# A decoder layer with attention and experts: first loads on two queues, where VectorE's large pieces lie in a step, and the order of the last output products

## Chip, cores and metric

The kernel runs on one core of a Trainium2 chip. The metric is the device time of one execution in microseconds; before the change the median of three runs is 1617.37 us (1615.99 to 1620.86). Traces come from one profiled execution of 1619.34 us, whose span from first to last instruction is 1617.6 us.

## What is computed

The input is x of shape (4, 512, 512): four batches of 512 rows, all in f32. The layer has three parts, each on a layer norm of the running sum:

```python
x = x + attention(layernorm(x), wq, wk, wv, wo)   # 32 query heads, 8 key heads of 64, rope, causal
x = x + quantized_product(layernorm(x), ctx)      # rows and ctx rounded to fp8 in blocks of 128
x = x + moe(layernorm(x), Wg, W1, W3, W2, sw1, sw3, sw2)

# moe, with T = 2048 rows, 8 experts, 256 places each, H = 704
eidx = argmax(softmax(xt @ Wg));  pos = place of the row in its expert's list
out  = gate * expert(eidx)(xt) if pos < 256 else 0
out += (silu(xt @ sw1) * (xt @ sw3)) @ sw2        # shared expert, for all rows
```

## The kernel before

**Engines.** TensorE (PE) does products and transposes, VectorE (DVE) and ScalarE (ACT) empty its banks, GpSimd (POOL) does rotation sums, divisions by softmax sums and additions to the running sum. Transfers are issued from ScalarE's queue (`bulk`, L102) and SP's queue. PSUM has 4 banks for scores and their transposes (`sp`), 1 for values' products (`av`), 3 for everything else (`mm`).

**The start** (L147 to L214, L1017 to L1043). Four row blocks of the first batch are loaded on ScalarE's queue, the rope tables on SP's, then weights of keys, queries and values. 40 dummy transposes (`spin`) run meanwhile. Then: statistics of the rows (`job_hs`), the rope tables' transposes into `rt`, 12 more dummies, then `job_h` (rows transposed), one key product, three query products and the first values' product.

**The step loop** (L1118 to L1133). Attention runs in 80 steps, 20 for each of the 4 batches; five steps treat four pairs of heads. Step `d` stands for two half steps `n = 2d` and `n + 1`. In a step the program writes down:

1. `scores` of the *next* step: the products of queries and keys into `sp` banks; VectorE takes each row's extreme and masks (`pm`, `mn`, L948), ScalarE takes exponentials (L958);
2. `weighted`: values' products of pairs that are ready (`av`, copied by ScalarE);
3. first half of the filler, `work.upto(n, ...)`;
4. `turned`: transposes of this step's probabilities (`pt`, L975), copied to `pT` by ScalarE (L986) and VectorE (L992);
5. second half of the filler, `work.upto(n + 1, ...)`.

Each engine takes its instructions in this written order.

**The filler.** All other work of the loop is cut into jobs: Python generators that write instructions and yield. Their keys: `q`, `k`, `v` (projections), `r` (reciprocals of softmax sums), `m` (their use on three quarters of a group), `o` (output product of a group of 8 heads), `c`, `cs` (rounding of ctx), `hs`, `h` (rows of the next batch), `s`, `t` (norm and quantized product), `w` (norm, router, scatter). The class `Fill` chooses: by due step, by what must be over (with a lag in halves of a step, `HALF` = 7250 ns), then by rank `want`. A yield of a positive number is time of TensorE in ns by the author's count; a negative one asks for a pause in halves; `"dve"` or `"quiet"` with a size asks for that much VectorE time in one piece, `"quiet"` also for GpSimd to be idle. `upto(n, pace, room, busy)` fills a half until TensorE's share `pace` is spent; pieces for VectorE are taken while `room` lasts (3.2 us in the first half, 4.4 in the second, L1127 and L1133). Jobs named in `CHAIN` (L720) are looked at first.

A group's output product `job_o` first writes the fourth quarter's division (`over_sums(b, a, 3)`), then pauses, then 16 products. It needs `wo`, whose tile has one buffer (L133), loaded once the group before is over.

**The tail.** After the loop, jobs left over are written between units of the shared expert (`units`, L1244 to L1267; `between` gives VectorE 2.5 us of room). When no job is left, three more units follow, then the experts, then what units remain, between groups of four rows that are gathered, combined and stored (L1353 to L1371). How many units remain depends on when the jobs end.

Of the kernel before, what the change touches and what calls it, by code (L numbers as in the profile page):

```python
# [8 lines left out]
F32 = mybir.dt.float32  # L9
# [14 lines left out]
def decoder_layer(  # L24
# [107 lines left out]
    def load_o(b, a):  # L132
        w = am2.tile([P, 4, D], F32, tag="wo", name=f"wo_{b}_{a}")  # L133
        bulk(
            out=w, in_=wo[a * 512 : (a + 1) * 512, :].rearrange("(r p) n -> p r n", p=P)
        )
        wts["o", a] = w
# [3 lines left out]
    def load_h(b):  # L141
        for j in range(TB):
            i = b * TB + j
            rows[b, j] = pj.tile([P, D], F32, tag="h", bufs=4, name=f"h_{b}_{j}")
            bulk(out=rows[b, j], in_=xf[i * P : (i + 1) * P, :])

    load_h(0)  # L147

    ident = const.tile([P, P], F32, name="ident")
# [12 lines left out]

    spin(40, "a")

# [15 lines left out]
    nc.sync.dma_start(out=rp, in_=rope.rearrange("(i p) c d -> p i c d", p=P))  # L180
    wts["v0"] = tile_v(0)
    load_k(0, 0)
    load_q(0, 0)
    load_v(0)

# [171 lines left out]
    def job_r(b, a):  # L357

        rr = am2.tile([P, 32], F32, tag="rr", bufs=2, name=f"rr_{b}_{a}")
        nc.vector.reciprocal(rr, rss[b, a])  # L360
        yield -0.6
        pt = bank("mm", f"prr_{b}_{a}")
        nc.tensor.transpose(pt[0:32, 0:P], rr, ident)
        rrT = am2.tile([32, P], F32, tag="rrT", bufs=2, name=f"rrT_{b}_{a}")
        nc.scalar.copy(rrT, pt[0:32, 0:P])
        yield 110
        n = b * NG + a
        bulk(out=rrd[n], in_=rrT)
        yield -0.6
        while n and over.get(("rrb", *divmod(n - 1, NG)), 1e18) + 0.7 * HALF > work.at:  # L370
            yield -0.2
        rrb = am2.tile([P, 4, T], F32, tag="rrb", name=f"rrb_{b}_{a}")
        rrbs[b, a] = rrb
        rows = rrd[n].rearrange("(r g i) q -> g r (i q)", r=4, g=2)
        for g in range(2):
            bulk(out=rrb[g * HD : (g + 1) * HD, :, :], in_=rows[g].partition_broadcast(HD))
# [5 lines left out]
    def job_m(b, a):  # L382
# [3 lines left out]
        yield 0  # L386

    def job_o(b, a):

        aT = aTs[b, a]  # L390
        over_sums(b, a, 3)
        over["rrb", b, a] = work.at
        yield -0.6
# [74 lines left out]
    def pace(b):  # L468

        return 1 if b < B - 1 else 0.5  # L470
# [33 lines left out]
    def job_c(b):  # L504
# [27 lines left out]
        for nt in range(TB + 1):  # L532
            if nt < TB:
                yield "quiet", 0.6, 2.4
                load_c(nt + 2)
                qs.append(quantize_round(vs[nt], f"c{b}_{nt}"))
                if nt < TB - 1:
                    scaled(nt + 1)
            else:
                yield -0.8  # L540
            if nt:
                turn(nt - 1)
                yield 220
# [11 lines left out]
    def job_t(b, j):  # L555
# [6 lines left out]
        block_max(am, h)  # L562
        yield "quiet", 0, 1.4
        inv, sx = block_scales(am, ACT_EPS, KC, f"x{b}_{j}", "x")
        cT, sw = cTs[b]

# [6 lines left out]
        )  # L573
        yield -0.5 * pace(b)
        v = quantize_scale(h, inv, f"x{b}_{j}")
        yield "quiet", 1 * pace(b), 2.4
        q = quantize_round(v, f"x{b}_{j}")
        yield -1 * pace(b)
        hT = bp.tile([P, KC, P], BF16, tag="h2T", bufs=2, name=f"h2T_{b}_{j}")
# [26 lines left out]
    def job_w(b):  # L606
# [14 lines left out]
        over["acc", b] = work.at  # L621
        yield -0.8 * pace(b)
        def small(tag, n=E, dt=F32):
# [95 lines left out]

    CHAIN = ("h", "hs", "cs", "c", "s", "t", "w")  # L720

# [16 lines left out]
    for b in range(B):  # L738
        z = b * SPB
        before = [(("acc", b - 2), 0.7)] if b > 1 else []  # L740
        add(z + 2, 0, ("x", b), load(load_x, b), *before)
        if b:
            add(z - 18, 0, ("wv", b), load(load_v, b), (("q", b - 1, 11), 0.5))
            add(z - 24, 0, ("hx", b), load(load_h, b), *([(("zero",), 0.7)] if b == 1 else []))
            add(z - 22, 0, ("hs", b), job_hs(b), (("hx", b), 1))
            add(z - 16, 1760, ("h", b), job_h(b), (("hs", b), 1), (("q", b - 1, 4 * NG - 1), 0))
        for j in range(TB):
# [5 lines left out]
        for a in range(NG):  # L753
# [17 lines left out]
            for r, due in enumerate((-9.5, -8.5, -7, -5)):  # L771
# [7 lines left out]
            n = b * NG + a  # L779
            before = [(("o", *divmod(n - 1, NG)), 0.7)] if n else []  # L780
            add(za + 5, 0, ("wo", b, a), load(load_o, b, a), *before)
            add(za + 7, 110, ("r", b, a), job_r(b, a))
            add(za + 8, 0, ("m", b, a), job_m(b, a), (("r", b, a), 1.5), want=za + 3)
            add(
                za + 10, 4 * MM4, ("o", b, a), job_o(b, a),
                (("wo", b, a), 1.5), (("x", b), 1), (("m", b, a), 0),
                want=za + (21, 21 if b < B - 1 else 18.5, 17, 16.5)[a],
            )
# [16 lines left out]
    class Fill:  # L805
# [4 lines left out]
        def first(self, n, room=0.0, chain=False):  # L810
            for i, job in enumerate(jobs):
                if job.key[0] in CHAIN:
                    if not room and self.at < self.cool:
                        continue
                elif chain:
                    continue
# [30 lines left out]

        def upto(self, n, pace, room=0.0, busy=0):

            self.cool = max(self.cool, self.at + busy)  # L850
            while True:

                spent, job = self.spent, self.first(n, room) if room > 0 else None
                if job:
# [3 lines left out]
                    if self.spent == spent:  # L858
                        continue
                elif self.spent >= pace:  # L860
                    return
                if self.spent < pace:

                    job = self.first(n, chain=True)
                    while job:
                        job = self.step(job, n)
                    if self.now is None:
# [152 lines left out]
    for c in range(2):  # L1020
        for half in range(2):
# [3 lines left out]
                rp[:, :, c, lo : lo + HH].unsqueeze(2).to_broadcast([P, TB, 2, HH]),  # L1025
            )
    rt = pj.tile([P, 2, T], F32, name="rt")
    for c in range(2):
# [7 lines left out]
        nc.scalar.copy(rt[:, c, :], pt)  # L1036
    spin(12, "b")
    for gen in (
        job_h(0), job_k(0, 0), job_q(0, 0), job_q(0, 1), job_q(0, 2), job_v(0, 0)
    ):  # L1040
        for _ in gen:
            pass
# [6 lines left out]

    even[B - 1] -= 4 * MM4 / SPB  # L1050

# [66 lines left out]
    for d in range(len(todo)):  # L1118
# [133 lines left out]
    def between():  # L1252
        work.at += 1720
        work.upto(n, 1e18, 2.5)

# [177 lines left out]
```

## Time and profile before

| what | value |
|---|---|
| median of three runs | 1617.37 us (1615.99 to 1620.86) |
| profiled execution, its span | 1619.34 us, 1617.6 us |
| granted TensorE clock over the span | 0.988 |
| step loop, first to last transposes of probabilities | 43.4 to 1100.7 us |
| experts | about 1323 to 1566 us |
| HBM traffic | 102 GB/s over the span |

The page's rows read: instruction group by line, engine, operation and tiles, count, busy us and mean ns; then the engine's idle time just before them and what ended it. Such rows for the operations that the change moves:

```profile
L443 DVE TENSOR_TENSOR qv_x<-qv_x,qm_x 128x512 f32<-128x512 f32 x16 | 16.8, 1048 | 0.6
L445 DVE TENSOR_TENSOR qq_x<-qv_x,qm_x 128x512 bf16<-128x512 f32 x16 | 15.3, 959 | 0.5
L568 DVE TENSOR_TENSOR sxw<-sf_c,sf_x 128x16 f32<-128x16 f32 x16 | 11.7, 728 | 0.6
L593 DVE TENSOR_TENSOR y<-py,sxw 128x512 f32<-128x512 f32 x64 | 42.9, 688 | 51.8 <-PE py L591 28.3 <-POOL acc L268 17.0 <-PE av L1006 3.7
```

A step is best read from a timeline of TensorE between two groups of `pt` transposes: sixteen records of about 0.11 us each.

### The profile page before, as it was taken

What the parts mean: (1) busy time and instruction counts of PE and PEld (TensorE: products, weight loads), DVE (VectorE), ACT (ScalarE), POOL (GpSimd) and SP (SyncE); (2) the same over time, 40 slices, a digit from 0 to 9 for tenths busy, and PEclk for the clock granted to TensorE, in tenths of its full rate; (3) what the DMA queues carried; (4) which work ended last, traced back from release to release, by engine and by line L of the source; (5) the groups of instructions that cost most, each with busy time, mean ns of one, the idle gap of its engine ahead of it and who ended that gap; (6) DMA issues with size and microseconds to landing.
All of it is one profiled execution on the core that took longest, in us unless ns stands there. A gap on an engine that the chain in (4) does not pass through costs nothing. (4 is left out here: it accounts for less than half of the span.)

```text
span 1617.6 us, 19823 instructions
## 1 busy us (share of the span) xinstructions
PE 1568.9 (97%) x6659; PEld 858.7 (53%) x6664; DVE 838.9 (52%) x2399; ACT 518.1 (32%) x1541; POOL 336.3 (21%) x293
## 2 busy tenths in 40 slices
PE   8999999999999998999999999989999999999998
PEld 5555554554545554454455554555444547767753
DVE  4466644478767456877745595765445211111113
ACT  2445443444444434333434444351100101101100
POOL 2031220214432030324303132322033000000012
PEclk9999999999999999999999999989999999999999
DMA  4373341353523253332515251246050253546427
GB/s 138 122 233 102 94 128 27 105 157 86 143 87 98 59 143 115 89 99 67 148 49 159 87 131 53 58 148 200 20 206 32 73 190 130 182 155 237 140 77 262
DMA packets 118918, 195.32 MB, mean 121 GB/s; under 512 B 17184, under 2 KB 36640, under 8 KB 118304
## 3 DMA queue, kind: packets, MB, share of 16 engines
q10 hardware_dynamic: 65760, 101.46, 21.7%
q1 hardware_dynamic: 50496, 84.20, 16.7%
q0 software_dynamic: 2560, 8.39, 1.6%
q8 instruction: 53, 0.87, 0.2%
q14 instruction: 49, 0.40, 0.1%
HBM read 136.07 MB, written 28.57 MB: 102 GB/s over the span
## 5 line engine op out<-in xcount | busy, mean ns | idle before, releaser
L958 ACT ACTIVATE pm<-pm,mn 128x256 f32<-128x256 f32 (+3 forms) x512 | 281.9, 553 | 362.4 <-DVE mn L948 322.8
L948 DVE CUSTOM_DVE_ANT_0 pm<-sc,mask 128x256 f32<-128x256 f32 (+3 forms) x512 | 217.1, 486 | 103.0 <-PE sc L925 102.7
L397 PE MATMUL py<-wo,aT 128*128 128x512 f32 x512 | 243.9, 610 | 3.2 <-POOL aT L268 1.7
L303 PE MATMUL psq<-hT,wq 128*128 128x512 f32 x512 | 236.6, 598 | 2.2 <-DVE y L593 1.7
L925 PE MATMUL sc<-kT,t1q 64*128 64x384 f32 (+3 forms) x1024 | 173.8, 455 | 12.8 <-DVE pT L992 5.5
L268 POOL TENSOR_TENSOR t1q<-t1q,tsq 128x512 f32<-128x512 f32 x64 | 83.5, 1305 | 437.5 <-DMA tsq<-t2q 243.6
L992 DVE COPY pT<-pt 128x128 f32<-128x128 f32 (+3 forms) x256 | 114.1, 485 | 108.8 <-PE pt L975 100.6
L975 PEld LDWEIGHTS pt<-ident,pm 128*128 128x128 f32 x1280 | 147.0, 143 | 39.3 <-issue 30.8
L975 PE MATMUL pt<-ident,pm 128*128 128x128 f32 x1280 | 156.4, 276 | 2.2 <-DVE pT L992 0.9
L986 ACT COPY pT<-pt 128x128 f32<-128x128 f32 (+3 forms) x256 | 98.6, 431 | 186.5 <-PE pt L975 160.2
L1006 PE MATMUL av<-pT,v 128*64 128x512 f32 (+3 forms) x1024 | 156.6, 448 | 0.0
L1167 PE MATMUL p_s<-h3x,slot_s 128*128 128x512 f32 x352 | 156.2, 595 | 0.0
L1167 PE MATMUL p_e<-xT,slot_e 128*128 128x256 f32 x704 | 155.1, 380 | 0.0
L303 PEld LDWEIGHTS psq<-hT,wq 128*128 128x128 f32 x512 | 91.7, 190 | 100.8 <-issue 95.8
L1167 PEld LDWEIGHTS p_e<-xT,slot_e 128*128 128x128 f32 x704 | 132.6, 190 | 23.2 <-issue 5.8
L397 PEld LDWEIGHTS py<-wo,aT 128*128 128x128 f32 x512 | 92.5, 192 | 96.0 <-issue 84.7
L925 PEld LDWEIGHTS sc<-kT,t1q 64*128 64x128 f32 x1024 | 87.5, 188 | 98.0 <-issue 64.7
L1006 PEld LDWEIGHTS av<-pT,v 128*64 128x64 f32 x1024 | 69.5, 139 | 110.5 <-issue 97.7
L268 POOL TENSOR_TENSOR acc<-acc,y 128x512 f32<-128x512 f32 x64 | 81.5, 1279 | 180.0 <-DVE y L593 179.0
L1167 PEld LDWEIGHTS p_s<-h3x,slot_s 128*128 128x128 f32 x352 | 65.5, 190 | 75.7 <-issue 73.7
L958 ACT ACTIVATION_READ_ACCUMULATOR pm<-pm,mn 128x1 f32 x512 | 96.9, 189 | 0.0
L268 POOL TENSOR_TENSOR aT<-aT,rrb 128x512 f32<-128x512 f32 x64 | 82.7, 1318 | 26.0 <-DMA rrb<-rrd 26.0
(174 smaller groups left out, 1362.7 us busy)
## 6 DMA issues: line engine op xcount, KB each, us to landing
slot_e<-in_L_ffn_W_dram SPq DMA_DIRECT2D x14, 1280.0 KB
wq<-in_L_attn_wq_dram ACTq DMA_DIRECT2D x16, 1024.0 KB
tsq<-t2q SPq DMA_DIRECT2D x256, 64.0 KB
wo<-in_L_attn_wo_dram ACTq DMA_DIRECT2D x16, 1024.0 KB
rrb<-rrd ACTq DMA_DIRECT2D x32, 512.0 KB
slot_e<-in_L_ffn_W_dram SPq DMA_DIRECT2D x7, 1408.0 KB
kT<-t1k ACTq DMA_DIRECT2D x64, 128.0 KB
xt<-x SPq DMA_DIRECT2D x28, 256.0 KB
```

Source lines behind the costliest of these rows:

```text
L268: nc.gpsimd.tensor_tensor(*args)
L303: nc.tensor.matmul(ps, w[:, k, c0 : c0 + P], hTs[b][:, k, :], start=(k == 0), stop=(k == KC - 1),)
L397: nc.tensor.matmul(py, aT[:, r, j * P : (j + 1) * P], wts["o", a][:, r, :], start=(r == 0), stop=(r == 3),)
L925: nc.tensor.matmul(scs[g][:, o : o + nk], qTs[b, p][g * HD : (g + 1) * HD, it * P : nk], kTs[b, p // 2][g * HD : (g + 1) * HD, 0:nk], star ...
L948: nc.vector.tensor_tensor_reduce(out=pm[:, o : o + nk], in0=scs[g][:, o : o + nk], in1=mask[:, T - nk : T], scale=-(HD**-0.5), scalar=3.0e ...
L958: nc.scalar.activation(pm[:, o : o + nk], pm[:, o : o + nk], AF.Exp, bias=mn, scale=-1.0, accum_out=rss[b, a][:, col : col + 1],)
L975: nc.tensor.transpose(pt[:, j * P : (j + 1) * P], pms[g][:, j * P : (j + 1) * P], ident)
L986: nc.scalar.copy(pT[:, 0 : it + 1, it * P : nk], pt[:, o : o + nk].rearrange("p (j t) -> p j t", t=P),)
L992: nc.vector.tensor_copy(pT[:, it + 1, 0:nk], pt[:, o : o + nk])
L1006: nc.tensor.matmul(av[g * HD : (g + 1) * HD, j * P : T], vs[b][:, j, v0 : v0 + HD], rhs, start=(j == 0), stop=(j == TB - 1),)
L1167: nc.tensor.matmul(pp[:, 0:cols], w13[:, k, o : o + P], xT[:, k, 0:cols], start=(k == 0), stop=(k == KC - 1),)
```

## The change

At the start, row blocks 1 and 3 of the first batch are loaded on SP's queue, ahead of the rope tables; the weights of values and keys are asked for right after the rows. The 12 later dummies join the first 40. The first batch's row transposes and first values' product are written before the rope tables' transposes.

In the loop, `upto` gets a limit `most` for one piece of VectorE: 1.35 us in the first half of a step, 9.0 in the second. Chain jobs are now looked at in each round, also when TensorE's share is spent, and with them jobs outside the chain that have no TensorE work left; `r`, `m` and the new `n` are chain jobs. `n` holds the fourth quarter's division, taken out of `job_o`. Sizes and pauses of several pieces are changed; the scale products `sxw` of a row block are written after its rounding.

For the last batch, the third group's output weights get a buffer of the values' tile, the order of its groups' output products is given by other ranks, and the share of filler per step is lowered by 7 products of 3.44 us rather than 4. In the tail VectorE's room is 2.8.

```diff
     def load_o(b, a):
-        w = am2.tile([P, 4, D], F32, tag="wo", name=f"wo_{b}_{a}")
+        if b == B - 1 and a == NG - 2:
+            w = am1.tile([P, 4, D], F32, tag="v", bufs=2, name=f"wo_{b}_{a}")
+        else:
+            w = am2.tile([P, 4, D], F32, tag="wo", name=f"wo_{b}_{a}")
...
-            bulk(out=rows[b, j], in_=xf[i * P : (i + 1) * P, :])
+            issue = nc.sync.dma_start if not b and j % 2 else bulk
+            issue(out=rows[b, j], in_=xf[i * P : (i + 1) * P, :])
     load_h(0)
+    wts["v0"] = tile_v(0)
+    load_v(0)
+    load_k(0, 0)
...
-    spin(40, "a")
+    spin(52, "a")
...
-    wts["v0"] = tile_v(0)
-    load_k(0, 0)
     load_q(0, 0)
-    load_v(0)
...
     def job_r(b, a):
+        late = 1 if b * NG + a < B * NG - 2 else 0.6
+        yield "dve", 0, 0.4
         nc.vector.reciprocal(rr, rss[b, a])
-        yield -0.6
+        yield -0.9 * late
...
-    def job_o(b, a):
-        aT = aTs[b, a]
+    def job_n(b, a):
         over_sums(b, a, 3)
         over["rrb", b, a] = work.at
-        yield -0.6
+        yield 0
+    def job_o(b, a):
+        aT = aTs[b, a]
...
-        yield "quiet", 0, 1.4
+        yield "quiet", 0, 1.0
         inv, sx = block_scales(am, ACT_EPS, KC, f"x{b}_{j}", "x")
+        yield -0.5 * pace(b)
+        v = quantize_scale(h, inv, f"x{b}_{j}")
+        yield "quiet", 1 * pace(b), 2.7
+        q = quantize_round(v, f"x{b}_{j}")
         cT, sw = cTs[b]
...
-        yield -0.5 * pace(b)
-        v = quantize_scale(h, inv, f"x{b}_{j}")
-        yield "quiet", 1 * pace(b), 2.4
-        q = quantize_round(v, f"x{b}_{j}")
-        yield -1 * pace(b)
+        yield -1.2 * pace(b)
...
-    CHAIN = ("h", "hs", "cs", "c", "s", "t", "w")
+    CHAIN = ("h", "hs", "cs", "c", "s", "t", "w", "r", "m", "n")
...
             before = [(("o", *divmod(n - 1, NG)), 0.7)] if n else []
+            if b == B - 1 and a > 1:
+                before = [(("o", b, 1), 0.7)] if a == 3 else []
...
-                (("wo", b, a), 1.5), (("x", b), 1), (("m", b, a), 0),
-                want=za + (21, 21 if b < B - 1 else 18.5, 17, 16.5)[a],
+                (("wo", b, a), 1.5), (("x", b), 1), (("n", b, a), 0.6),
+                want=za + ((21, 21, 17, 16.5) if b < B - 1 else (22, 19.5, 18, 16.5))[a],
...
-                elif chain:
+                elif chain and job.left > 0:
                     continue
...
-        def upto(self, n, pace, room=0.0, busy=0):
+        def upto(self, n, pace, room=0.0, busy=0, most=9.0):
...
-                spent, job = self.spent, self.first(n, room) if room > 0 else None
+                spent, job = self.spent, self.first(n, min(room, most)) if room > 0 else None
...
-                elif self.spent >= pace:
+                job = self.first(n, chain=True)
+                if job is None and self.spent >= pace:
                     return
+                while job:
+                    job = self.step(job, n)
...
-    spin(12, "b")
-    for gen in (
-        job_h(0), job_k(0, 0), job_q(0, 0), job_q(0, 1), job_q(0, 2), job_v(0, 0)
-    ):
+    for gen in (job_k(0, 0), job_q(0, 0), job_q(0, 1), job_q(0, 2)):
...
-    even[B - 1] -= 4 * MM4 / SPB
+    even[B - 1] -= 7 * MM4 / SPB
...
-        work.upto(n, goal, 3.2, 1900)
+        work.upto(n, goal, 3.2, 1900, 1.35)
...
-        work.upto(n, 1e18, 2.5)
+        work.upto(n, 1e18, 2.8)
```

Left out are pauses in `job_c` (0.8 to 1.3) and `job_w` (0.8 to 1.2), a later load of the running sum, and earlier ranks for `r` and `m`; and that `job_h(0)` and `job_v(0, 0)` now run ahead of the tables' transposes.

More of the change, by code (lines that the diff above doesn't have):

```diff
@@ L368, in job_r @@
         bulk(out=rrd[n], in_=rrT)
-        yield -0.6
+        yield -0.6 * late
         while n and over.get(("rrb", *divmod(n - 1, NG)), 1e18) + 0.7 * HALF > work.at:
@@ L386, in job_m @@
         yield 0
+    def job_n(b, a):
+        over_sums(b, a, 3)
+        over["rrb", b, a] = work.at
+        yield 0
     def job_o(b, a):
         aT = aTs[b, a]
-        over_sums(b, a, 3)
-        over["rrb", b, a] = work.at
-        yield -0.6
         for j in range(TB):
@@ L539, in job_c @@
             else:
-                yield -0.8
+                yield -1.3
             if nt:
@@ L621, in job_w @@
         over["acc", b] = work.at
-        yield -0.8 * pace(b)
+        yield -1.2 * pace(b)
         def small(tag, n=E, dt=F32):
@@ L740, in decoder_layer @@
         before = [(("acc", b - 2), 0.7)] if b > 1 else []
-        add(z + 2, 0, ("x", b), load(load_x, b), *before)
+        add(z + 5, 0, ("x", b), load(load_x, b), *before)
         if b:
@@ L745, in decoder_layer @@
             add(z - 22, 0, ("hs", b), job_hs(b), (("hx", b), 1))
-            add(z - 16, 1760, ("h", b), job_h(b), (("hs", b), 1), (("q", b - 1, 4 * NG - 1), 0))
+            add(z - 16, 1760, ("h", b), job_h(b), (("hs", b), 1.5), (("q", b - 1, 4 * NG - 1), 0))
         for j in range(TB):
@@ L780, in decoder_layer @@
             before = [(("o", *divmod(n - 1, NG)), 0.7)] if n else []
+            if b == B - 1 and a > 1:
+                before = [(("o", b, 1), 0.7)] if a == 3 else []
             add(za + 5, 0, ("wo", b, a), load(load_o, b, a), *before)
-            add(za + 7, 110, ("r", b, a), job_r(b, a))
-            add(za + 8, 0, ("m", b, a), job_m(b, a), (("r", b, a), 1.5), want=za + 3)
+            add(za + 7, 110, ("r", b, a), job_r(b, a), want=za - 20)
+            add(za + 8, 0, ("m", b, a), job_m(b, a), (("r", b, a), 1.5 if n < B * NG - 2 else 1), want=za - 20)
+            add(za + 10, 0, ("n", b, a), job_n(b, a), (("m", b, a), 0), want=za - 20)
             add(
                 za + 10, 4 * MM4, ("o", b, a), job_o(b, a),
-                (("wo", b, a), 1.5), (("x", b), 1), (("m", b, a), 0),
-                want=za + (21, 21 if b < B - 1 else 18.5, 17, 16.5)[a],
+                (("wo", b, a), 1.5), (("x", b), 1), (("n", b, a), 0.6),
+                want=za + ((21, 21, 17, 16.5) if b < B - 1 else (22, 19.5, 18, 16.5))[a],
             )
@@ L859, in upto @@
                         continue
-                elif self.spent >= pace:
+                job = self.first(n, chain=True)
+                if job is None and self.spent >= pace:
                     return
+                while job:
+                    job = self.step(job, n)
                 if self.spent < pace:
-                    job = self.first(n, chain=True)
-                    while job:
-                        job = self.step(job, n)
                     if self.now is None:
@@ L1026, in decoder_layer @@
             )
+    for gen in (job_h(0), job_v(0, 0)):
+        for _ in gen:
+            pass
     rt = pj.tile([P, 2, T], F32, name="rt")
```

## Prediction

> **What bounds the kernel now.** I read the page's busy shares first, then windows of TensorE, then its timeline at the worst windows. The share says that TensorE is the bound, and also how little there is to win: 1617.6 - 1568.9 = 48.7 us idle.
>
> ```profile
> PE 1568.9 (97%) x6659; PEld 858.7 (53%) x6664; DVE 838.9 (52%) x2399; ACT 518.1 (32%) x1541; POOL 336.3 (21%) x293
> ```
>
> Idle is not the whole loss: after gaps the granted clock halves for a while. To count both I took a rule from the trace. I cut the step loop (80 steps, numbered from 0) at the first transpose of each step's probabilities (`pt`, L975) and counted, from the order of TensorE's instructions, the filler between two cuts: a product 128x512 in f32 costs 0.86 us (two records of 429 ns), in bf16 0.22, a row block's four transposes 0.44 or 0.22. An undisturbed step lasts filler + 6.16 us (scores 2.1, values' product 2.3, transposes 1.75), or 3.86 in each fifth step, which has no values' product. The next view gives busy us by engine, then the clock: rows 1 and 4 are undisturbed steps (11 fillers, 9.46 + 6.16 = 15.62), the others the worst.
>
> ```profile
> core 0: us, PE busy (x) PEld busy (x) DVE busy (x) ACT busy (x) POOL busy (x), PEclk, DMA share, GB/s
> 241.25:256.87 15.62, 15.62 (x68) 7.94 (x67) 6.15 (x19) 5.85 (x18) 0.00 (x0) 1.00 0.23 50
> 629.33:647.27 17.94, 12.76 (x57) 6.58 (x57) 10.27 (x41) 8.26 (x28) 2.31 (x2) 0.81 0.27 87
> 658.01:678.65 20.64, 17.89 (x75) 8.56 (x74) 18.31 (x39) 7.42 (x25) 11.27 (x9) 0.92 0.25 56
> 1018.59:1034.21 15.62, 15.62 (x67) 7.77 (x66) 12.70 (x30) 5.29 (x16) 5.92 (x5) 1.00 0.23 52
> 1050.11:1059.14 9.03, 6.71 (x50) 4.48 (x48) 8.88 (x16) 1.53 (x4) 5.33 (x4) 1.00 0.09 32
> 1059.14:1067.55 8.41, 7.07 (x32) 4.98 (x33) 5.66 (x26) 7.90 (x29) 0.00 (x0) 0.80 0.61 202
> 1067.55:1081.42 13.87, 12.72 (x45) 6.63 (x47) 5.01 (x20) 6.82 (x23) 0.00 (x0) 0.63 0.63 182
> 1081.42:1088.97 7.55, 7.04 (x48) 4.44 (x47) 5.33 (x17) 4.86 (x15) 2.55 (x2) 1.00 0.40 123
> ```
>
> Row 4 is busy on VectorE (12.70 of 15.62) and loses nothing; the last rows are not and lose most. So what matters is whether TensorE has filler while it waits, and what stands ahead of the evacuations that it waits for. In the window at 629.33 (step 44, one 0.11 us filler) TensorE's timeline shows:
>
> ```profile
> 629.33 1.91 PE L975 MATMUL pt<-ident,pm 128*128 128x128 f32 x16
> 633.91 1.63 PE L925 MATMUL sc<-kT,t1q 64*128 64x256 f32 x10 [2.68 <-DVE pT L992]
> 638.05 2.07 PE L925 MATMUL sc<-kT,t1q 64*128 64x128 f32 x6 [2.50 <-DVE mn L948]
> ```
>
> VectorE did the 13 small operations of a root before the copies `pT`, then a row's scales before the next maxima `mn`.
>
> Losses by the rule (duration - filler - constant, router products counted too), 66.8 us: steps 74 to 77 38.9 - 23.5 = **15.3** (almost no filler left); 44: 17.94 - 9.60 = **8.3**; 46, 49, 51: **12.9**; 35, 36, 55, 56: **9.5** (transposes wait behind exponentials on ScalarE); 65, 70, 71: **4.4**; twelve small ones in 1 to 33, 52, 53: **16.4**. Outside: at the start TensorE waits for the first rows; at the end DMA and VectorE outlast it:
>
> ```profile
> 12.04 2.09 PE L252 MATMUL ptr_h<-ident,h 128*128 128x128 f32 x16 [2.32 <-DVE h L246]
> 14.87 3.70 PE L303 MATMUL psk<-hT,wk 128*128 128x512 f32 x8 [0.74 <-ACT hT L294]
> ...
> 1609.61 2.17 DVE L1344 SCALAR_TENSOR_TENSOR xt<-og,gk,xt 128x512 f32<-128x512 f32 x3 [2.06 <-DMA xt<-x]
> 1612.18 0.75 DVE L1344 SCALAR_TENSOR_TENSOR xt<-og,gk,xt 128x512 f32<-128x512 f32 x1 [0.40 <-DMA xt<-x]
> 1612.85 1.28 DVE L1236 TENSOR_TENSOR xt<-ys,xt 128x512 f32<-128x512 f32 x2
> ```
>
> **Part 1, the start: -0.8 us.** Row statistics run at 4.71, 6.44, 7.27, 8.06; only the second really waits, and at VectorE's pace (0.8 a row) they would end at 8.0, not 8.94: 0.9 gained. The Trainium skill speaks against it (DMA: Bandwidth & Descriptors, Issuing engines are not separate DMA queues): transfers from several engines share the same 16 DMA engines, only issue time is saved. By that rule two rows of issue, 2 x 0.52, are the ceiling, and no bandwidth comes; by the rows, 0.9. They nearly agree in size, for another reason: the rope tables now stand behind the rows on SP's queue instead of beside them. The values' product needs one transposed row block, so the 0.74 wait goes. Against: the rope transposes (1.04, idle time before) now stand between products, about -0.87. Sum 0.9 + 0.74 - 0.87 = 0.8. The first key product starts at about 17.5 (13.2 + 3.44 + 0.87) against 14.87, 2.6 later, the first scores 0.8 earlier; the second pair's rotation was there at 31.73, now about 34.3, and is wanted at about 33.7: at most 0.6 lost. Ends 0 and -1.5. The 12 dummy transposes are moved, not added.
>
> **Part 2, filler near the loop's end: -13.** Output products of the last batch's third group now lie in steps 76 to 78, where there was none (its weights get the values' second buffer, so their 1 MB load needn't wait for the second group), and two query products in 74 and 75. Steps 74 to 78 hold 4.3 to 5.6 us each; 75 to 77 held 0.0 to 0.4. Steps with 4 or more lose nothing before; I keep 2 of the 15.3.
>
> **Part 3, large VectorE pieces late: -21 of 35.** No planned piece over 1.35 us stands ahead of the copies any more. Step 44's root moves behind the copies; with 0.11 filler it still loses what 14 and 24 lose with such filler, 1.6 to 1.8, and some backlog: 2.7. In 46, 51, 26, 31 a quantized row was transposed or added too soon; now an output product or two stand before: 46, 49, 51 keep 2. In 35, 36, 55, 56 the transposes move to the late half: 0.5 left. 65, 70, 71 keep 1. The small ones: 26, 31, 20 go (4.0), 4 and 24 grow by 1.3 and 1.2 (filler of 1.83 goes; a scales piece of 2.0 comes), and late pieces (4.5 to 6.3 us of VectorE against 3.4 to 3.9 of filler in 9, 27, 29, 49) make the next maxima late, and with them PSUM banks: +4. So 18 for 16.4. The work of scale products moved behind rounding (728 ns each while GpSimd runs) is hidden on VectorE: nothing.
>
> **Part 4, a new stall after the last step: +3.7.** In its late half VectorE gets a statistic, a reciprocal, a root (13 x 0.17), four 0.66 normalisations and an addition, 6.7 us, ahead of the copies `pT` that the last values' product waits for; TensorE has 3 output products (2.6), that step's values' product (2.3) and transposes (1.75) beside it. VectorE reaches the copies' end near 18.5 us after the last scores, TensorE wants them at 14.8. No row shows this exact place; ends 0 (VectorE ahead) and 6 (GpSimd stretches it).
>
> **Clock: +3.** The Trainium skill (TensorE: Matmul & The Clock Gate, Why this matters for your kernels) puts a drop at idle gaps over about 3 us. Here gaps of 2.35 (513) and 2.38 (806) were followed some 14 us later by 3.41 us at half clock, while 2.50 (734) was not. By the rule only part 4's gap costs, 1.7; by the rows step 44's does too: 2 x 1.7. I take the rows, 3. Another 4 for waits that the order doesn't show.
>
> **Part 5, the tail: +4.4.** The chain's jobs end one shared-expert unit later, so one unit (16 x 0.43 = 6.9) stands before the experts rather than after. The end doesn't give it all back: four-row groups take turns of out, load, gather and combine (combines at 1580.9, 1592.2, 1601.9, 1609.6), about 10 us each. With one unit fewer, four combines (4 x 0.75) and outputs stand behind the last additions. I lay the end 48.9 us after the experts' last product, 51.3 now: 2.4 back of 6.9. Ends 2 and 6.
>
> **Sum.** Losses left: 2 + 2.7 + 2 + 0.5 + 1 + 18 + 3.7 + 3 + 4 = 36.9, saved 66.8 - 36.9 = 29.9. Span 1617.6 - 29.9 - 0.8 + 4.4 = 1591.3, or 1593.0 for the profiled execution (1619.34). Against the runs' median 1617.37: **1591**.
>
> **Rivals.** (a) The filler comes, but late maxima and banks take back half of the gain: 1617 - 13 = 1605; for it, only three PSUM banks serve all filler; against, steps 29 and 30 had 3.5 late and 4.4 early and lost 0.9. (b) Slower: the same lateness at every quantizing piece. About 22 of them in the loop (3.2 us each) move behind the copies; a wait of 1.4 us at each eats the 29.9 in full, and at 1.6 the time is 1622. Against: in 35 and 55 6.9 us already stood there before long filler. (c) Steps lose as little as those with the same filler did, no new stall: 1578. That the change doesn't do what it says is out for the filler: the order shows it.
>
> **Chances.** Forecast 0.70, (a) 0.14, (b) 0.08, (c) 0.08. The forecast's own span is 1581 to 1602 (ends of parts 1, 4, 5 and of the 4 + 3); taking in most of (a) and (c): 1577 to 1609. Within 0.3% (4.9 us, what can be told from no change): the rim of (a), 0.04; faster 0.88, slower 0.08.
>
> **What would show it.** Windows from 1000 to 1090 at clock 1.00 and no gap over 1 us; step 44 below 13 us; first key product about 17.5 us, first values' product near 13.2; a TensorE wait for `pT` of 3 to 4 us before the last `av`; the last combines after the last `ys` additions. Wrong if `py` or `psq` wait for VectorE in many steps, or if the tail past 1090 shows gaps.

## The result and the profile after

The changed kernel takes **1592.36 us** (median of four runs, 1591.37 to 1595.72) beside 1616.68 (1614.32 to 1620.86) for the kernel before in runs on the same chip: a ratio of 0.985, 95% interval 0.9825 to 0.9876. The forecast was 1591, with 1577 to 1609 as its range. The profiled execution took 1592.05 us, its span 1590.3 against 1617.6. The busy shares of the page say as little as before: TensorE's busy time fell by 14.9 us, the span by 27.3.

```profile
PE 1554.0 (98%) x6664; PEld 853.4 (54%) x6664; DVE 822.6 (52%) x2399; ACT 515.0 (32%) x1541; POOL 333.4 (21%) x293
```

The next view cuts the changed kernel's span into the stretches that answer to those shown of before (us, busy us of each engine with its number of instructions, granted clock, DMA share, GB/s): an undisturbed step, step 44, step 46, steps 74 to 77 one by one, and three pieces behind the loop.

```profile
core 0: us, PE busy (x) PEld busy (x) DVE busy (x) ACT busy (x) POOL busy (x), PEclk, DMA share, GB/s
241.66:257.28 15.62, 15.62 (x68) 7.94 (x67) 6.07 (x19) 5.74 (x18) 0.44 (x1) 1.00 0.21 46
628.17:638.99 10.82, 9.92 (x59) 5.89 (x58) 9.68 (x42) 7.90 (x28) 1.33 (x2) 1.00 0.09 24
649.84:666.00 16.16, 16.16 (x74) 8.41 (x73) 13.68 (x34) 4.56 (x17) 10.61 (x9) 1.00 0.29 69
...
1017.83:1029.60 11.77, 11.77 (x68) 6.65 (x66) 8.41 (x27) 6.58 (x22) 0.00 (x0) 1.00 0.44 92
1029.60:1035.97 6.37, 6.37 (x41) 3.97 (x40) 3.98 (x10) 2.33 (x5) 4.63 (x4) 1.00 0.19 42
1035.97:1050.15 14.18, 13.85 (x64) 6.70 (x63) 11.14 (x35) 7.99 (x29) 12.13 (x11) 1.00 0.33 105
1050.15:1061.45 11.30, 11.30 (x58) 5.84 (x57) 5.49 (x18) 5.28 (x16) 1.33 (x2) 1.00 0.99 333
1068.29:1088.30 20.01, 18.31 (x77) 9.79 (x76) 11.06 (x22) 6.19 (x11) 1.04 (x1) 1.00 0.94 263
1088.30:1090.60 2.30, 0.11 (x1) 0.12 (x2) 0.00 (x0) 0.58 (x1) 1.43 (x2) 1.00 0.78 231
1090.60:1094.00 3.40, 3.40 (x5) 1.29 (x6) 0.00 (x0) 0.00 (x0) 3.40 (x3) 0.50 0.01 2
```

The undisturbed step is the same 15.62. Step 44 went from 17.94 to 10.82, step 46 from 20.64 to 16.16, and in 74 to 77 TensorE is busy to within 0.33 us, at full clock. The last two rows are new: an idle stretch and then half a clock, behind the loop.

TensorE's timeline of step 44 (start, duration, engine, line, operation, count, and in brackets the idle time before it and what ended it) has one short wait where there were two of over 2.5:

```profile
628.19 1.97 PE L989 MATMUL pt<-ident,pm 128*128 128x128 f32 x16
...
631.17 2.07 PE L939 MATMUL sc<-kT,t1q 64*128 64x256 f32 x16 [0.90 <-ACT pT L1000]
```

The loop also has one new wait of over 2 us. It lies in step 40, which lost nothing before and loses 2.4 us now. TensorE's timeline first, then lines from GpSimd's and VectorE's:

```profile
589.09 1.96 PE L408 MATMUL py<-wo,aT 128*128 128x512 f32 x4 [2.14 <-issue]
```

```profile
581.96 4.93 POOL L273 TENSOR_TENSOR aT<-aT,rrb 128x512 f32<-128x512 f32 x4
...
585.73 1.19 DVE L710 TENSOR_TENSOR r_dst<-r_dst,spill 128x4 f32<-128x4 f32 x1
...
588.30 0.68 DVE L319 TENSOR_TENSOR t1q<-psq,rt 128x512 f32<-128x512 f32 x1
```

In the kernel before, the same operations of the router ran while GpSimd was idle (VectorE's timeline):

```profile
570.62 0.16 DVE L699 TENSOR_TENSOR r_dst<-r_dst,spill 128x4 f32<-128x4 f32 x1
```

Five such operations took 1.1 to 1.2 us each, 5.9 in all for 0.8 before, and the copies of the query products stood behind them. The output product started 0.1 us after the last of these copies. That it waited for the bank is read from this order; the profile names no releaser.

**Where the 27.3 us of the span come from.** Cut at the same three events (first and last `pt`, first `epy`), the two traces give:

| stretch | before | after | difference |
|---|---|---|---|
| start to the loop's first transposes | 43.44 | 44.50 | +1.1 |
| step loop | 1057.2 | 1023.8 | -33.4 |
| loop's last transposes to the experts' first output product | 252.1 | 258.5 | +6.3 |
| from there to the end | 264.8 | 263.6 | -1.3 |

The loop took 7.0 us more filler with it (544.5 for 537.5), so its losses fell by 40.4. Of the third row, 6.9 is one shared-expert unit that now stands before the experts, 7.0 is output products that have gone into the loop, and the remaining 6.4 is mostly two waits, 3.9 together, and 1.7 of half clock.

The start lost time where it should have gained. TensorE's timeline there, and the clock in the same stretch (columns as in the windows above):

```profile
11.60 3.35 PE L257 MATMUL ptr_h<-ident,h 128*128 128x128 f32 x16 [2.47 <-DVE h L251]
14.74 3.93 PE L350 MATMUL psv<-wv,hT 128*128 128x512 f32 x8
18.51 1.04 PE L1048 MATMUL prt<-ident,rsrc 128*128 128x128 f32 x8
19.38 3.67 PE L308 MATMUL psk<-hT,wk 128*128 128x512 f32 x8
```

```profile
8.60:12.00 3.40, 0.93 (x9) 0.69 (x7) 3.05 (x13) 0.00 (x0) 1.42 (x4) 1.00 1.12 332
12.00:15.40 3.40, 3.40 (x16) 3.05 (x15) 0.91 (x2) 2.17 (x4) 0.00 (x0) 0.50 0.43 158
```

The first four row blocks' transposes took 3.35 us where they had taken 2.09: half a clock from 12.0 to 15.4, at once behind the wait.

Behind the loop two waits stand on TensorE, the last step's `pT` and the fourth group's division by the softmax sums; the second is GpSimd's, and GpSimd itself waited for a transfer (second block: GpSimd's timeline, then ScalarE's queue, where that transfer was issued):

```profile
1071.88 2.81 PE L1020 MATMUL av<-pT,v 128*64 128x512 f32 x16 [1.68 <-ACT pT L1000]
...
1090.49 3.68 PE L408 MATMUL py<-wo,aT 128*128 128x512 f32 x4 [2.20 <-POOL aT L273]
```

```profile
1089.17 3.70 POOL L273 TENSOR_TENSOR aT<-aT,rrb 128x512 f32<-128x512 f32 x3 [11.50 <-DMA rrb<-rrd]
...
1076.14 1.33 ACTq L384 DMA_DIRECT2D rrb<-rrd  x2
```

The reciprocals were transposed at 1068.2 and came back, spread over the partitions, at 1089.2, 21 us later. The first 8 us passed before the read back was issued at 1076.1; the other 13 lie in a stretch with the DMA engines 94% busy. How much of them that traffic caused, no run tried.

At the end VectorE's last pieces, from its timeline, are combines of routed rows that wait for transfers; the last four stand behind the shared expert's last additions (`ys`):

```profile
1579.01 1.28 DVE L1250 TENSOR_TENSOR xt<-ys,xt 128x512 f32<-128x512 f32 x2
1582.56 2.17 DVE L1358 SCALAR_TENSOR_TENSOR xt<-og,gk,xt 128x512 f32<-128x512 f32 x3 [2.26 <-issue]
1585.38 0.75 DVE L1358 SCALAR_TENSOR_TENSOR xt<-og,gk,xt 128x512 f32<-128x512 f32 x1 [0.66 <-DMA xt<-x]
```

### The profile page after: what moved, and what is told of

Read it like the earlier page. It is cut to its first block, busy times and chain, and to the rows that moved or that the text cites. A ratio compares the mean times of both kernels' runs of the same rounds, so it can differ in the third digit from the quotient of the medians.

```text
span 1590.3 us, 19839 instructions
## 1 busy us (share of the span) xinstructions
PE 1554.0 (98%) x6664; PEld 853.4 (54%) x6664; DVE 822.6 (52%) x2399; ACT 515.0 (32%) x1541; POOL 333.4 (21%) x293
## 4 chain that ended last, share of the span: by engine, by line
PE 87%; DMA 4%; DVE 3%; POOL 2%; ACT 1%; issue 1%; SPq 1%; ACTq 0%; DVEq 0%; POOLq 0%
PE py L408 14%; PE psq L308 13%; PE p_e L1181 10%; PE p_s L1181 9%; PE sc L939 8%; PE av L1020 8%; PE pt L989 7%; PE epy L1209 4%; PE psv L350 4%; PE ys L1209 3%; PE psk L308 3%; PE ptr_h L257 1%; DMA xt<-x 1%; DMA tsq<-t2q 1%; ACT pm L972 1%
## 5 line engine op out<-in xcount | busy, mean ns | idle before, releaser
L408 PE MATMUL py<-wo,aT 128*128 128x512 f32 x512 | 240.3, 603 | 4.6 <-POOL aT L273 2.2
L939 PE MATMUL sc<-kT,t1q 64*128 64x384 f32 (+3 forms) x1024 | 165.8, 448 | 6.3 <-ACT pT L1000 2.5
L989 PEld LDWEIGHTS pt<-ident,pm 128*128 128x128 f32 x1280 | 143.7, 141 | 36.8 <-issue 27.8
L1020 PE MATMUL av<-pT,v 128*64 128x512 f32 (+3 forms) x1024 | 152.4, 439 | 1.7 <-ACT pT L1000 1.7
```

The lines of the kernel that those rows point to most:

```text
L408: nc.tensor.matmul(py, aT[:, r, j * P : (j + 1) * P], wts["o", a][:, r, :], start=(r == 0), stop=(r == 3),)
L939: nc.tensor.matmul(scs[g][:, o : o + nk], qTs[b, p][g * HD : (g + 1) * HD, it * P : nk], kTs[b, p // 2][g * HD : (g + 1) * HD, 0:nk], star ...
L989: nc.tensor.transpose(pt[:, j * P : (j + 1) * P], pms[g][:, j * P : (j + 1) * P], ident)
L1020: nc.tensor.matmul(av[g * HD : (g + 1) * HD, j * P : T], vs[b][:, j, v0 : v0 + HD], rhs, start=(j == 0), stop=(j == TB - 1),)
```

## The experiments

Theory after the two traces: the middle's gain is the limit of 1.35 us, the loop's end is gained by the third group's products, and start and tail cost time. Rivals are named with each run. "Loop", "tail" and "end" below are the stretches of the table above; losses of groups of steps are counted by the prediction's rule in each trace.

**1. Without the limit.**

```diff
-        work.upto(n, goal, 3.2, 1900, 1.35)
+        work.upto(n, goal, 3.2, 1900)
```

> The changed kernel without the limit of 1.35 us on planned VectorE pieces ahead of the copies; all else stays. Theory (the limit makes the gain of the middle): steps 44, 46, 49, 51, 35, 36, 55 and 56 lose again about what they lost in the kernel before, 30.7 in sum against 4.3 now, so +20 to +26 us: 1612 to 1618 us; step 44 near 17 us long, its first wait at the copies pT over 2 us. Rival (the longer pauses and the first place for the softmax sums' jobs made it): within 5 us of the changed kernel, 1592 to 1597, steps 46, 49, 51 still losing under 2.

Measured 1608.74 us (1606.14 to 1610.99), 0.9923 of before (0.9897 to 0.9949): 16.4 us slower than the changed kernel. The loop grew by 20.2 and the tail shrank by 3.9. Losses: step 44 4.3 (1.1 with the limit), 46, 49 and 51 7.8 (1.3), 74 to 77 4.8 (1.1); 33 and 53, which the theory had not named, 3.8 and 4.3 (0.65). But 35, 36, 55 and 56 lost only 0.3 (1.9), and step 40 nothing (2.4). One wait of TensorE, from its timeline, shows what the limit keeps away:

```profile
773.67 1.11 PE L257 MATMUL ptr_h<-ident,h 128*128 128x128 f32 x4 [3.63 <-ACT hT L299]
```

So the limit matters, somewhat less than thought. The gain at 35 and 55 does not need it: the rest of the change brings it too, as does the limit by itself (run 2). And the new wait in step 40 is not there without the limit.

**2. The limit alone, in the kernel before.**

```diff
-        def upto(self, n, pace, room=0.0, busy=0):
+        def upto(self, n, pace, room=0.0, busy=0, most=9.0):
...
-                spent, job = self.spent, self.first(n, room) if room > 0 else None
+                spent, job = self.spent, self.first(n, min(room, most)) if room > 0 else None
...
-        work.upto(n, goal, 3.2, 1900)
+        work.upto(n, goal, 3.2, 1900, 1.35)
```

> The kernel before with only the limit of 1.35 us added. Theory: the middle's 26 us are gained, the 15 us of steps 74 to 77 stay lost, and one more shared-expert unit stands before the experts, as in the changed kernel (+5.6): 1617 - 26 + 5.6, about 1597, between 1592 and 1603. Rival (the limit needs the longer pauses, without them late pieces only move the wait to the maxima): 1606 to 1617, with steps 46, 49, 51 still losing over 2 us each.

Measured 1615.29 us (1612.43 to 1617.60), 0.997 of before (0.995 to 0.999). The rival's time, but not for its reason: the loop is 18.4 us shorter, with 46, 49 and 51 losing 2.6 and 35, 36, 55 and 56 1.9. Step 44 still loses 6.0: its root now stands behind the copies, but ahead of the next maxima, and the half clock stays. Steps 74 to 77 still lose some 14. The tail is 14.2 longer: the unit of 6.9, 1.7 of filler that moved out of the loop, and 5.6 left, of which TensorE's waits in the trace make 4.4; its timeline shows the two largest:

```profile
1111.14 8.85 PE L1167 MATMUL p_s<-h3x,slot_s 128*128 128x512 f32 x20 [1.82 <-ACT gT L1178]
...
1122.59 1.12 PE L397 MATMUL py<-wo,aT 128*128 128x512 f32 x2 [1.73 <-POOL aT L268]
```

What is put off in the steps piles up behind the loop. The limit's gain was kept only where the rest of the change stood beside it.

**3. Without the part for the loop's end.**

```diff
-        if b == B - 1 and a == NG - 2:
-            w = am1.tile([P, 4, D], F32, tag="v", bufs=2, name=f"wo_{b}_{a}")
-        else:
-            w = am2.tile([P, 4, D], F32, tag="wo", name=f"wo_{b}_{a}")
+        w = am2.tile([P, 4, D], F32, tag="wo", name=f"wo_{b}_{a}")
...
-            if b == B - 1 and a > 1:
-                before = [(("o", b, 1), 0.7)] if a == 3 else []
...
-                want=za + ((21, 21, 17, 16.5) if b < B - 1 else (22, 19.5, 18, 16.5))[a],
+                want=za + (21, 21 if b < B - 1 else 18.5, 17, 16.5)[a],
...
-    even[B - 1] -= 7 * MM4 / SPB
+    even[B - 1] -= 4 * MM4 / SPB
```

> The changed kernel with the part for the loop's end undone (third group's weights back in the single buffer, its old dues and wants, share of the last batch as before). Theory: steps 74 to 77 lose some 10 to 13 us again, with 0 to 0.65 of filler in two of them and a half clock after: 1602 to 1606. Rival (the filler is only moved, and what is won before 1068 is lost again behind it, where the changed kernel waits 1.7 and 2.2 us and runs 3.4 us at half clock): 1592 to 1596, with no wait of 2 us at the fourth group's first output product.

Measured 1598.80 us (1597.88 to 1599.38), 0.9867 of before (0.9844 to 0.9889): 6.4 slower than the changed kernel, between the two. Both mechanisms act: steps 74 to 77 lose some 10 (1.1) and the loop is 10.0 longer, and behind it 5.3 are won back, since there is no wait over 0.3 us left there and no half clock.

**4. The old start.** Rows on one queue, the keys' product first, 40 and 12 dummies; the diff is the start's part of the change, reversed.

> The changed kernel with the old start (rows on one queue, keys' product first, 12 dummy transposes after the rope transposes). Theory from the two traces: the new start costs 1.07 us (first transposes of the loop at 44.50 against 43.44), so 1591.3, 1 us faster than the changed kernel, with the first scores' transposes at 43.4. Rival (the prediction's part 1): the new start gains 0.8, so 1593.2. Third: step 2 or 3 holds other work with it, which a difference over 2 us would show.

Measured 1595.87 us (1592.96 to 1599.90), 0.9848 of before (0.9819 to 0.9878): not distinguishable from the changed kernel by the intervals, and on the other side than the theory. The first transposes did come at 43.5, 1.0 sooner, but the loop took 1.6 more, the tail 0.9 and the end 3.0. Of the loop's 1.6, 1.4 is half clock behind the wait in step 40, which did not follow in the changed kernel's trace. Runs 9 and 10 come back to the start.

**5. The softmax sums' jobs not first.**

```diff
-    CHAIN = ("h", "hs", "cs", "c", "s", "t", "w", "r", "m", "n")
+    CHAIN = ("h", "hs", "cs", "c", "s", "t", "w")
...
-                elif chain and job.left > 0:
+                elif chain:
```

> The changed kernel with the softmax sums' jobs (r, m, n) no longer counted to the chain of jobs that go first, and with the old rule for a chain's free jobs; the part for the loop's end, the limit and the pauses stay. Theory (the order of TensorE shows it): the third group's output products fall back behind step 77, the filler in the loop is 537.6 us instead of 544.5, steps 75 to 77 hold 0.2, 0.1 and 0.4 of it and lose 12 to 15 us again; the 6.9 of filler then stand behind the loop, where the two waits of 1.7 and 2.2 us go: 1597 to 1604. Rival (the buffer and the dues alone bring the filler to the loop's end): 1590 to 1594.

Measured 1609.65 us (1603.98 to 1613.73), 0.9951 of before (0.9938 to 0.9965): 17.3 slower than the changed kernel, far more than the theory gave. Steps 74 to 77 lose only 5.6. The rest is spread: the loop holds 6.9 less filler and is still 12.8 longer, with 5.1 lost in step 24, 4.0 in 60 and 3.9 in 70. Two of these steps in TensorE's timeline:

```profile
861.00 4.49 PE L308 MATMUL psq<-hT,wq 128*128 128x512 f32 x6 [2.11 <-DVE qv_c L454]
```

```profile
989.43 0.28 PE L371 MATMUL prr<-ident,rr 128*32 128x128 f32 x1 [1.14 <-DVE y L604]
990.50 3.66 PE L308 MATMUL psq<-hT,wq 128*128 128x512 f32 x4 [0.78 <-ACT rrT L373]
```

In the second the reciprocals' transposes stand in TensorE's order before VectorE and ScalarE are ready for them. How the sums' place leads to each of the other waits I did not trace further.

**6. The old pauses.** 0.8 for 1.3 before the attention rows' transposes, 1 for 1.2 before the quantized rows', 0.8 for 1.2 before the router's scores.

```diff
-                yield -1.3
+                yield -0.8
...
-        yield -1.2 * pace(b)
+        yield -1 * pace(b)
...
-        yield -1.2 * pace(b)
+        yield -0.8 * pace(b)
```

> The changed kernel with the old pauses in front of the transposes of the attention rows (0.8 for 1.3), of the quantized rows (1.0 for 1.2) and before the router's scores (0.8 for 1.2). Theory: the limit of 1.35 us and the order of the jobs carry the middle, and TensorE's order changes only in steps 32, 33, 47, 49, 52, 53 and 61: 1590 to 1596, steps 46, 49, 51 together under 3 us of loss. Rival (the limit alone brought 3 us and not 26 because of the short pauses): over 1600, with waits for VectorE of over 1.4 us at transposes in several steps.

Measured 1593.02 us (1591.71 to 1594.21), 0.985 of before (0.9817 to 0.9882): the time of the changed kernel, but not its course. The loop is 4.2 us longer: 46, 49 and 51 lose 4.0 instead of 1.3, over the theory's 3, and step 40 1.2 more. It does not show in the time because one shared-expert unit stands behind the experts again. TensorE's timelines behind the last expert, first the changed kernel, then this run, show its 16 products (56 for 40):

```profile
1540.12 17.43 PE L1181 MATMUL p_s<-h3x,slot_s 128*128 128x512 f32 x40
...
1538.17 24.30 PE L1181 MATMUL p_s<-h3x,slot_s 128*128 128x512 f32 x56
```

The tail is 6 us shorter for it and the end 1.9 longer. So this run compares two changes at once. Beside run 7, where the unit also stands behind, it is 7.6 us slower: 1.6 of that at the start by half clock, 3.4 in the loop and 2.7 in the tail, in the profiled pair.

**7. The unit back behind the experts.**

```diff
-    for _ in range(3):
+    for _ in range(2):
         f, *args = units.pop(0)
```

> The changed kernel with two shared-expert units instead of three before the experts, so that the unit of 6.9 us stands after them again as in the kernel before. Theory: the experts start 6.9 us sooner and the end, set by the last combines and transfers, grows by only 1.3 (50.7 to 52.0): 1592.4 - 5.6, about 1587 (1585 to 1589). Rival (the rows of the first experts aren't there by then, TensorE waits at their transposes): 1591 to 1593, with a wait of some 5 us there.

Measured **1585.42 us** (1582.81 to 1588.75), 0.9803 of before (0.9774 to 0.9832): 6.9 faster than the changed kernel; no wait at the experts' first rows. In its trace the tail is 8.8 shorter (the unit, and no half clock there) and the end 1.9 longer. Of the 7.7 us between the two profiled executions, 1.6 comes from a faster start, though nothing was changed there (why, the last section tells):

```profile
11.54 2.09 PE L257 MATMUL ptr_h<-ident,h 128*128 128x128 f32 x16 [1.79 <-DVE h L251]
```

**8. Three repairs.**

```diff
-    spin(52, "a")
+    spin(72, "a")
...
-                (("wo", b, a), 1.5), (("x", b), 1), (("n", b, a), 0.6),
+                (("wo", b, a), 1.5), (("x", b), 1), (("n", b, a), 0.6 if n < B * NG - 1 else 1.0),
...
-    for _ in range(3):
+    for _ in range(2):
         f, *args = units.pop(0)
```

> The changed kernel with three repairs: the unit back behind the experts; the last group's output products due 0.4 of a half step later after their division; 72 instead of 52 dummy transposes at the start. Theory: -5.6 for the unit, -2.2 for the wait of the first output product on the division and -1.7 for the 3.41 us at half clock behind it, -1.7 for the 3.41 us at half clock at 12.0: 1592.4 - 11.2, about 1581 (1580 to 1584). Rival (the waits only move to the next thing that VectorE and GpSimd owe): 1585 to 1588, no better than the unit alone; and the 20 transposes may delay the first row's transposes (first transposes of the loop later than 44.5).

Measured **1582.33 us** (1581.22 to 1583.82), 0.9782 of before (0.9755 to 0.981). That is 10.0 faster than the changed kernel against 11.2 expected, and 3.1 faster than the unit alone. The product no longer waits for the division; a wait of 1.1 for the running sum has come in its place (TensorE's timeline), which is the rival's mechanism at a part of the price:

```profile
1088.64 1.88 PE L408 MATMUL py<-wo,aT 128*128 128x512 f32 x4
...
1095.25 0.66 PE L257 MATMUL ptr_h<-ident,h 128*128 128x128 f32 x4 [1.09 <-DVE acc L416]
```

The start in windows: the dummies left 0.7 us idle there instead of 2.5, and the clock stays up.

```profile
8.60:12.00 3.40, 2.67 (x25) 2.42 (x23) 3.09 (x12) 0.00 (x0) 1.42 (x4) 1.00 1.11 334
12.00:15.40 3.40, 3.40 (x20) 2.28 (x18) 0.88 (x2) 2.05 (x4) 0.00 (x0) 1.00 0.39 142
```

**9 and 10. The old start once more, beside the three repairs.** Run 9 is the kernel of run 8 with the old start of run 4, run 10 that of run 8 unchanged, both on one chip.

> The changed kernel with the unit back and the later output products of the last group, and with the old start (rows on one queue, keys' product first, 40 and 12 dummy transposes). Theory (the new start is 0.6 us sooner by itself, first transposes of the loop at 42.9 against 43.5, and the changed kernel lost that only by 3.41 us at half clock at 12.0): 0.6 us slower than the three repairs of the same call, about 1583. Rival (the new start is worth more than its first 45 us show, because the old one shifts the work of steps 2 to 11): 2 us slower or more, as the 3.5 us of the earlier undoing had it.

> The kernel with the three repairs again, beside the one with the old start: 1582 us within 1.5, first transposes of the loop at 42.9, and 0.6 us faster than the old start (rival: 2 or more).

Measured 1586.94 us (1586.54 to 1590.76) with the old start and 1582.93 (1582.70 to 1584.88) with the new one; ratios 0.9819 (0.9797 to 0.9841) and 0.979 (0.9769 to 0.9811). No run of one reaches into those of the other: the new start is worth about 4.0 us, which is the rival's size, but not its reason: the loop took 1025.6 us in both. The profiled executions differ by only 2.1: 1.4 up to the loop (42.8 against 44.2) and 1.8 in the end stretch, less 1.0 in the tail. Why the end is longer with the old start (266.8 against 265.1 us here, 266.5 in run 4 against 263.6 in the changed kernel) the traces did not tell; that stays open.

No run undid the other parts alone: the changed sizes of pieces, the place of `sxw`, the longer lag ahead of the rows' transposes, and the tail's room of 2.8.

## Why the prediction was right

The time was right to 1.4 us. The loop's mechanism held nearly to the number; behind it the closeness is luck, since errors cancel: in the span, 4.3 us less was lost behind the loop and to the unforeseen than allowed, against 1.9 more at the start and 1.2 more for the tail. By its own steps:

- **Parts 2 and 3, the loop.** Losses of 66.8 were to shrink to 26.2 (2 + 2.7 + 2 + 0.5 + 1 + 18), by 40.6; they shrank by 40.4. Groups: 74 to 77 keep 1.1 (2 forecast), step 44 1.1 (2.7), 46, 49 and 51 1.3 (2), 35, 36, 55 and 56 1.9 (0.5), 65, 70 and 71 4.0 (1). All other steps together lose about 17, some 0.6 more than before (1.6 forecast), but for other reasons: the late pieces in 9, 27, 29 and 49 cost little, and step 40's new wait, which nobody forecast, costs 2.4. What the runs correct is the ascription. The filler near the loop's end comes only with the softmax sums' jobs first (run 5), which the prediction spoke of nowhere, and the limit alone brings 2.8 us (run 2).
- **Part 4, the wait after the last step.** Forecast 3.7, measured 1.7; VectorE did stand behind a root, four normalisations and an addition. Missed was the next wait, 2.2 for the fourth group's division, for the reciprocals' way through the DRAM, whose read back was issued late and landed 13 us after that.
- **Clock.** Forecast 3, as two drops of 1.7: one after step 44, one behind part 4. In the loop, 34.1 us at half clock before, ten windows of 3.41, became none, so up to 17 of the 40.4 us saved are clock and the rest waits. The trace has one at the start and one after the second wait: 2 x 1.7, right in size and wrong in both places. Wrong too was the reading that the drop comes "some 14 us later". Windows of the kernel before put it at once behind the wait that ended at 515.8:

```profile
core 0: us, PE busy (x) PEld busy (x) DVE busy (x) ACT busy (x) POOL busy (x), PEclk, DMA share, GB/s
...
513.40:516.60 3.20, 0.85 (x6) 0.68 (x6) 3.10 (x6) 2.82 (x10) 1.93 (x2) 1.00 0.28 63
516.60:520.00 3.40, 3.40 (x6) 1.23 (x6) 1.18 (x1) 1.17 (x2) 0.63 (x1) 0.50 0.55 154
```

- **The 4 us for unforeseen waits** were not needed in the loop. Part 4, clock and this allowance were 10.7; behind the loop 6.4 was lost.
- **Part 1, the start.** Forecast -0.8, in the profiled pair +1.1. The last row statistics ended at 8.0 as foreseen, and the product of the values runs without the 0.74 wait; but the first key product came at 19.4, not 17.5, since the wait for the normalised rows fell so that half a clock followed. Where it did not (runs 7, 8 and 10), the key product of run 8 starts at 17.8 and the loop 0.5 to 0.6 sooner than before. Over whole executions the new start is worth about 4.0 (runs 9 and 10), so the term was too small, in part for a difference at the other end of the kernel that stays unexplained.
- **Part 5, the tail.** Forecast +4.4 as 6.9 less 2.4; the end gave back 1.3, so +5.6. The last combines do stand behind the last additions. Run 7 shows the term alone: with the unit put back, the tail is 8.8 shorter (6.9, and 1.7 of half clock) and the end 1.9 longer, 5.2 for the unit itself.
- **Hidden work.** The scale products `sxw` were costed at nothing; they became cheaper (309 ns each on average for 728).

Rival (a), half of the gain given back by banks and late maxima, did not come; what there is of it lies in step 40 and in step 24, which lost 1.4 more. Rival (b), a wait at each late piece, fell with it. (Its 1622 leaves out the 3.6 us of start and tail; with them it is 1626.) Rival (c), no new stall, failed behind the loop and in step 40. Of step 44 the prediction says 0.11 us of filler; its own sum of 9.60 rightly counts 3.4 us of key products with it.

Removed one at a time, the limit is worth 16.4 us, the sums' first place 17.3, the loop's end 6.4, the start 3.5 (4.0 in the repaired kernel), and the pauses 0.7, a figure that hides the unit of run 6. Their sum, 44, is well over the 24.3 of all together. The limit is worth 16.4 beside the other parts and 2.8 alone. The sums' first place alone was not run.

## What to carry to other kernels

Putting large pieces late in a step paid little here by itself: look behind the loop for what was postponed, and for the short jobs that end in a transfer. When two runs take the same time, check that the same work stands in the same phases before calling a part worthless (run 6). When work is moved across a phase, cost the units that move with it: one unit of 6.9 us, moved by the rule that starts the experts once no job is left, cost 5 to 6 us here, and one number gave them back. Before filling a wait with dummies, look at its length: what one trace shows of the clock behind it may be the luck of that execution.

## What the hardware showed

**The clock goes by fixed windows.** In each of the twelve traces every stretch at half clock begins on one grid of 3.413 us (to 0.05% of a window), whose phase differs from execution to execution (0.78 and 2.27 us from the span's start in runs 8 and 10, which are one kernel). I counted TensorE's idle time in each window up to 1400 us: of 21 windows with 2.0 us or more idle, all were followed by a window at half clock; of 60 with 1.2 to 2.0, 11; of 4823 with less, 5, of which four prolonged a half clock already running. So a wait's place decides as well as its length. The wait in step 40, 1.8 to 2.2 us long in the eight traces that have it at this output product, was followed by half clock in five (runs 3, 4, 6, 7 and 9). At the start the luck lies earlier still: full clock came at 5.2 us in the changed kernel's trace and at 6.4 in run 7's, so that there the same 52 dummies ended 0.6 later, the wait behind them was 1.79 instead of 2.47 us, and no half clock followed. In run 9 a wait of 2.97 us, from 9.8 to 12.8, crossed a border of the grid (at 11.5), left the clock at 1.00 on both sides, and cost only itself; that of 2.47 in the changed kernel lay in one window and cost 1.7 more, half of the 3.41 us that follow. The windows also explain what the prediction noted without a reason, that waits of 2.35 and 2.38 us were followed by half clock and one of 2.50 (734.0 to 736.5) was not: a border at 735.0 split it, and the two windows hold 1.3 and 1.5 us idle. The Trainium skill (TensorE: Matmul & The Clock Gate, What's actually happening) has the free-running window of 3.413 us, and these runs agree with it; the bound of about 3 us of idle that the prediction weighed is too high here.

```profile
core 0: us, PE busy (x) PEld busy (x) DVE busy (x) ACT busy (x) POOL busy (x), PEclk, DMA share, GB/s
...
8.60:12.00 3.40, 1.22 (x12) 0.98 (x9) 2.92 (x17) 0.54 (x2) 0.00 (x0) 1.00 1.05 382
12.00:15.40 3.40, 2.09 (x16) 1.68 (x16) 2.06 (x5) 1.93 (x4) 0.00 (x0) 1.00 0.56 207
```

These are run 9's windows at the start: 2.2 and 1.3 us idle in cuts of 3.40 laid as in the other kernels; its own grid lies otherwise, and no half clock follows.

**A small VectorE operation can last as long as what GpSimd does beside it.** `sxw` took 728 ns on average in the kernel before and 309 in the changed one, but no single one took either. In the kernel before, ten of the 16 began while GpSimd was in an instruction, took 0.97 to 1.18 us, and ended 0.03 us after it; the other six took 0.17 to 0.18. Two of these, from the timelines:

```profile
636.24 1.04 POOL L268 TENSOR_TENSOR qv_x<-h,iv_x 128x512 f32<-128x512 f32 x1 [4.54 <-DVE sf_x L463]
636.27 1.04 DVE L568 TENSOR_TENSOR sxw<-sf_c,sf_x 128x16 f32<-128x16 f32 x1
...
651.80 0.17 DVE L568 TENSOR_TENSOR sxw<-sf_c,sf_x 128x16 f32<-128x16 f32 x1
```

Behind the rounding only two of 16 were caught so, at 1.24 and 1.36 us; one more, which began within 0.01 us of GpSimd's instruction, was not. This was worth 6.7 us of VectorE and none on the path. In step 40 the router's operations were caught in the same way, and there it cost TensorE 2.1 us.
